# Two levels of Strassen for two of three feed-forward products, with their sums made during attention

## The chip, the core and the metric

The kernel runs on one core of a Trainium2 chip. The metric is the device time of one execution in microseconds, as the median of several runs. The program is one launch: inputs and output lie in HBM, everything between in the core's own memories (SBUF and PSUM) or in HBM scratch tensors of the kernel.

## What is computed

A transformer block with gated slot attention and a gated feed-forward part, on x of shape (2, 2048, 512), all in float32. Of the reference this matters here:

```python
x = layernorm(x + attention(x, Wq, Wk, Wv, Wg, Ws, Wo, g_norm_weight))
up_gate = einsum('bsd,hd->bsh', x, W1)      # W1: 2048 x 512
up_lin  = einsum('bsd,hd->bsh', x, W3)      # W3: 2048 x 512
hidden  = silu(up_gate) * up_lin
hidden  = fwht(hidden)                      # Walsh-Hadamard over the 2048 hidden channels
out     = einsum('bsh,dh->bsd', hidden, W2) # W2: 512 x 2048
x = layernorm(x + out)
```

The Hadamard transform is linear, so the kernel applies it once to W2 and leaves `hidden` as it is.

## The kernel before, in words

**Strassen's form.** A product of two matrices cut into 2 x 2 quarters needs eight products of quarters; Strassen's form (in Winograd's variant) needs seven, of quarters and of sums of quarters. Every large product here is made that way once. Each left factor is kept as seven slots (`LEFT`, line 91, says which slot product k reads), each right factor too (`RIGHT`), and `SUM` says in which of three PSUM sums product k is accumulated: products 1, 6, 7 and 4 go into c1, one after the other, and each of the partial sums on the way is read before the next product is added on top; 5 and 3 go into c2, 2 into c3. So product 6 may not start before the sum after product 1 was read, 7 not before that after 6, and 4 not before that after 7. In this document such a wait from one product of c1 to the next is a hop.

**Attention** (lines 114 to 672). Four groups of four heads (NG = 4), and in each group 16 steps of 128 tokens of both batch rows: 64 steps. `run(new, now, before, old)` (line 557) writes out one step's instructions by hand for TensorE (PE), VectorE (DVE), ScalarE (ACT) and GpSimd (POOL), under `manual_schedule`, so these four engines take their instructions in exactly this order. It interleaves four steps: `new` loads and (in the first group) transposes tokens (`load_x`, `make_x`), `now` makes q, k, s and v and the scores, `before` makes the values, `old` adds its output product to the residual rows (`o`, line 474), in the last group normalises them (`row_stats`, `store_rows`) and writes them to the HBM tensor yd. Transfers are issued by SyncE (SP), whose order a scheduler sets. PSUM has eight banks: `ps[0]` and `ps[1]` with two each for scores and transposes, and four for the sums of `Unit` (line 203): c1 twice, c2 and c3 once.

**W2's preparation** is a generator, `hadamard()` (line 505), which is advanced at three places of each step from the second group on: after `make_x`, after `row_stats`, and ahead of `store_rows`. It loads a tile, transposes it, multiplies it with a 128 x 128 Hadamard matrix, makes four stages of sums (`stage`, lines 516 and 517: two DVE additions of 1024 elements; one stage in every third place), forms Strassen's seven slots and stores them in the HBM tensors w2s.

**Feed-forward** (lines 675 to 860), under the scheduler's own order. Four blocks of eight row tiles (1024 tokens). `load_tokens` reads a block's rows from yd, transposes them and makes the seven slots. For each of eight pairs of hidden blocks, `up` makes W1's and W3's seven products each, with 512 columns (`product`, line 747), W1's and W3's turn about, so two chains of c1 alternate; ACT copies some sums (`keep`, line 754), DVE adds others (`add`, line 759), `combine` (line 764) makes the silu with a tanh on ACT and two DVE operations, and POOL makes the sums that W2's product needs. The weights' slots are made in the first block from W1 and W3 (`load_weights`, line 710, with transposes on PE) and kept in HBM (w13s); later blocks load them. `down` (line 799) makes W2's product for four pairs at a time, each of its seven products with four multiplications of 256 columns, and adds it to the residual rows (line 824), normalised after the second call.

Of the kernel before, what the change touches and what calls it, by code (L numbers as in the profile page):

```python
# [8 lines left out]
F32 = mybir.dt.float32  # L9
AF = mybir.ActivationFunctionType  # L10
ALU = mybir.AluOpType
# [15 lines left out]
NPB = NFB // 2  # L27
HD = D // 2
EPS = 1e-5
# [4 lines left out]
def gated_slot_attention_ffn_kernel(  # L34
# [20 lines left out]
    of = out.rearrange("b t d -> (b t) d")  # L55

# [38 lines left out]
    w13s = [dram.tile([P, 2, 7, 2, P], F32, name=f"w13s{p}") for p in range(NPB)]  # L95
# [15 lines left out]
    with ExitStack() as att:  # L111
        wp = att.enter_context(tc.tile_pool(name="wp", bufs=1))
        xp = att.enter_context(tc.tile_pool(name="xp", bufs=2))
        yp = att.enter_context(tc.tile_pool(name="yp", bufs=7))
# [28 lines left out]
        class Weights:  # L143


            def __init__(self, name, parts, raw=None):
                width = sum(p[1] for p in parts)
                self.t = wp.tile([P, 7, 2, width], F32, name=name)
# [36 lines left out]
        def load_o(g):  # L185
            def scaled(a):

                nc.gpsimd.tensor_scalar(a, a, gn, 0.5, ALU.mult, ALU.mult)

            at = g * HG * DV  # L190
            return Weights("wo_", [(lambda j: wo[at + 2 * j * DV : at + (2 * j + 2) * DV, :], HD)], scaled)

# [308 lines left out]

# [3 lines left out]
        def hadamard():  # L505

            for pair in ((0, 2), (1, 3)):
                wh = [hp.tile([P, NFB, P], F32, name=f"wh{i}") for i in range(2)]
                ping = hp.tile([P, NFB, P], F32, name="ping")

                def stage(i, s):

                    src, dst = (wh[i], ping) if s % 2 == 0 else (ping, wh[i])
                    a = src.rearrange("p (a two s) d -> p a two s d", two=2, s=1 << s)
                    o = dst.rearrange("p (a two s) d -> p a two s d", two=2, s=1 << s)
                    nc.vector.tensor_tensor(o[:, :, 0], a[:, :, 0], a[:, :, 1], ALU.add)
                    nc.vector.tensor_tensor(o[:, :, 1], a[:, :, 0], a[:, :, 1], ALU.subtract)

                for i, dt in enumerate(pair):
                    for q in range(NFB // 4):  # L520
                        raw = yp.tile([P, D], F32, name="raw", tag="rows")
                        nc.sync.dma_start(out=raw, in_=w2[dt * P : (dt + 1) * P, q * D : (q + 1) * D])
                        yield
                        for c in range(4):
                            nc.tensor.transpose(bank(0)[:, c, :], raw[:, c * P : (c + 1) * P], ident)
                        t0 = hp.tile([P, 4, P], F32, name="t0")
                        nc.scalar.copy(t0, bank(0))
                        yield
                        nc.tensor.matmul(bank(2), lhsT=hm, rhs=t0, start=True, stop=True)
                        nc.scalar.copy(wh[i][:, 4 * q : 4 * q + 4, :], bank(2))  # L530
                        yield
                for i in range(2):
                    for s in range(4):
                        stage(i, s)
                        for _ in range(3):
                            yield
                j = pair[0] * P
                for hb in range(NPB):
                    b11, b21, b12, b22 = (wh[i][:, hb + h * NPB] for i in range(2) for h in range(2))
                    wt = hp.tile([P, 4, P], F32, name="wt")  # L540
                    nc.vector.tensor_tensor(wt[:, 0], b12, b11, ALU.subtract)
                    nc.gpsimd.tensor_tensor(wt[:, 2], b22, b12, ALU.subtract)
                    nc.vector.tensor_tensor(wt[:, 1], b22, wt[:, 0], ALU.subtract)
                    nc.gpsimd.tensor_tensor(wt[:, 3], b21, wt[:, 1], ALU.subtract)
# [3 lines left out]
                    nc.sync.dma_start(out=o[:, 3:7], in_=wt)  # L548
                    yield
# [3 lines left out]
        w2_work = hadamard()  # L553
# [3 lines left out]
        def run(new, now, before, old):  # L557
# [23 lines left out]
            prepare = new is not None and new.g > 0  # L581
            if prepare:
                next(w2_work, None)
# [7 lines left out]
            if prepare:  # L591
                next(w2_work, None)
# [6 lines left out]
            if prepare:  # L599
                next(w2_work, None)  # L600
# [53 lines left out]
            if last:  # L654
                nw["qks"].sums(3)

        with tc.manual_schedule(
# [13 lines left out]
            for _ in w2_work:  # L671
                pass


    xp = ctx.enter_context(tc.tile_pool(name="fxb", bufs=1, reuse_waits="tile"))
    rawp = ctx.enter_context(tc.tile_pool(name="fraw", bufs=3, reuse_waits="tile"))
    hp = ctx.enter_context(tc.tile_pool(name="fhid", bufs=5, reuse_waits="tile"))
    wp = ctx.enter_context(tc.tile_pool(name="fw13", bufs=2, reuse_waits="tile"))
    w2p = ctx.enter_context(tc.tile_pool(name="fw2", bufs=4, reuse_waits="tile"))
    tmp = ctx.enter_context(tc.tile_pool(name="ftmp", bufs=2, reuse_waits="tile"))  # L680
    rp = ctx.enter_context(tc.tile_pool(name="fres", bufs=1, reuse_waits="tile"))
    ptp = ctx.enter_context(tc.tile_pool(name="ptp3", bufs=2, reuse_waits="tile", space=PSUM))
    pch = ctx.enter_context(tc.tile_pool(name="pch", bufs=2, reuse_waits="tile", space=PSUM))
    NBLK = NCH // 8
    TH = 4 * P
    GP = 4

    def load_tokens(blk):

        xb = xp.tile([P, 7, 2, TH], F32, name="xb")  # L690
        b12 = xp.tile([P, 2, TH], F32, name="b12")
# [207 lines left out]
```

## Time and profile before

| | us |
|---|---|
| median of three runs | 3827.41 (3825.83 to 3828.25) |
| the profiled execution | 3831.67 |
| its span, first to last instruction | 3829.9 |
| PE busy in the span | 3765.3 |
| DVE busy | 1983.0 |
| ACT busy | 966.5 |
| POOL busy | 806.4 |
| attention, from the start to its last PE product | 2608.5 |
| the rest, feed-forward | 1221.4 |

In a group's row of the profile stand the line, the engine, the operation, out<-in, the shapes and the count; then the busy time in us and the mean of one instruction in ns; then the time for which the engine was idle just ahead of these instructions, and what ended most of that wait. PE executes a float32 multiplication as two instructions, so each program-level multiplication is counted twice. In the chain of work in order of time, a line has the start, the length and the work; in the timeline, start, length and instruction, with the idle time and its releaser in brackets.

### The profile page before, as it was taken

Reading aid. Unit: us, or ns where it says so; the run is one execution under the profiler, and the core shown is the slowest. Engines: PE = TensorE matmul, PEld = TensorE weight load, DVE = VectorE, ACT = ScalarE, POOL = GpSimd, SP = SyncE. Lnnn points to the kernel's source line nnn. Section 1 sums busy time; section 2 is a strip of 40 time slices with the busy share of each in tenths; the row PEclk is TensorE's granted clock in tenths of the full one; section 3 lists DMA queues with packets and bytes.
Section 4 is the critical chain, followed back from the end, with each engine's and each line's share of the span. In section 5 each row is a group of like instructions: output and inputs, shape, how many; then the busy total and the mean of one; then the engine's idle time right before and its main releaser. Section 6 shows DMA issues by size and latency. Waiting matters only on the chain.

```text
span 3829.9 us, 57893 instructions
## 1 busy us (share of the span) xinstructions
PE 3765.3 (98%) x24416; PEld 2657.8 (69%) x24416; DVE 1983.0 (52%) x3020; ACT 966.5 (25%) x1621; POOL 806.4 (21%) x821
## 2 busy tenths in 40 slices
PE   9999999999999999999999999997999999999999
PEld 7777777677777777777777777774566466466466
DVE  5555555555655655546666666563434334334334
ACT  2322222222222222232222222222211211211211
POOL 2222221211212222112122222222311211212211
PEclk9999999999999999999999999998999999999999
DMA  4112113111121321111221211104323224223220
GB/s 142 56 53 79 53 57 107 60 57 59 42 74 48 100 79 48 60 59 42 74 88 63 78 53 61 47 25 170 121 88 124 77 77 143 77 77 119 93 77 22
DMA packets 124579, 290.19 MB, mean 76 GB/s; under 512 B 13600, under 2 KB 52640, under 8 KB 120224
## 3 DMA queue, kind: packets, MB, share of 16 engines
q1 hardware_dynamic: 124320, 286.50, 22.1%
q8 instruction: 192, 3.15, 0.3%
q14 instruction: 67, 0.55, 0.0%
HBM read 207.68 MB, written 78.64 MB: 75 GB/s over the span
## 4 chain that ended last, share of the span: by engine, by line
PE 94%; DVE 2%; DMA 1%; issue 1%; POOL 1%; ACT 0%; SPq 0%; POOLq 0%; DVEq 0%; ACTq 0%
PE c L301 20%; PE c L749 20%; PE c L271 16%; PE c L484 10%; PE c L817 9%; PE ps L427 3%; PE ps L363 2%; PE ps L410 2%; PE ps L348 2%; PE ps L468 1%; PE ps L329 1%; PE ps L415 1%; PE ps L433 1%; PE ps L351 1%; DMA raw<-in_L_ffn_W 1%
## 5 line engine op out<-in xcount | busy, mean ns | idle before, releaser
L301 PE MATMUL c<-wvg,xb 128*128 128x512 f32 x1792 | 863.8, 605 | 0.0
L749 PE MATMUL c<-xb,w 128*128 128x512 f32 x1792 | 776.3, 594 | 0.7 <-ACT w L725 0.7
L749 PEld LDWEIGHTS c<-xb,w 128*128 128x128 f32 x1792 | 339.6, 191 | 417.3 <-issue 406.9
L271 PE MATMUL c<-xb,wqks 128*128 128x128 f32 x3584 | 557.1, 278 | 7.0 <-DVE rows L480 2.0
L271 PEld LDWEIGHTS c<-xb,wqks 128*128 128x128 f32 x3584 | 491.1, 193 | 29.2 <-DVE rows L480 3.6
L301 PEld LDWEIGHTS c<-wvg,xb 128*128 128x128 f32 x1792 | 310.8, 190 | 266.4 <-issue 257.2
L817 PE MATMUL c<-w2t,hid 128*128 128x256 f32 x1792 | 392.5, 379 | 3.9 <-DVE res L824 3.9
L817 PEld LDWEIGHTS c<-w2t,hid 128*128 128x128 f32 x1792 | 338.3, 190 | 53.0 <-DVE res L824 6.3
L224 ACT COPY kept<-c 128x384 f32<-128x384 f32 (+1 forms) x384 | 203.0, 529 | 651.3 <-PE c L271 497.3
L271 PE MATMUL c<-wqks,xb 128*128 128x128 f32 x1792 | 348.5, 276 | 0.9 <-DMA wqks<-in_L_attn_Ws 0.9
L229 DVE TENSOR_TENSOR t<-c,kept 128x384 f32<-128x384 f32 (+1 forms) x384 | 230.4, 601 | 195.1 <-PE c L271 194.6
L761 DVE TENSOR_TENSOR out<-c,kept 128x512 f32<-128x512 f32 x192 | 131.7, 686 | 339.3 <-PE c L749 339.3
L480 DVE TENSOR_TENSOR rows<-c,rows 128x256 f32<-128x256 f32 x448 | 182.1, 417 | 188.3 <-PE c L484 186.6
L271 PEld LDWEIGHTS c<-wqks,xb 128*128 128x128 f32 x1792 | 273.7, 193 | 1.2 <-DMA wqks<-in_L_attn_Ws 1.2
L756 ACT COPY kept<-c 128x512 f32<-128x512 f32 x192 | 112.4, 585 | 599.0 <-PE c L749 599.0
L288 POOL TENSOR_TENSOR e<-e,zc 1x512 f32<-1x512 f32 x60 | 75.8, 1264 | 782.8 <-ACT e L287 782.8
L340 DVE RECIPROCAL iz<-z 128x256 f32<-128x256 f32 x128 | 223.6, 1747 | 20.9 <-ACT z L331 20.9
L824 DVE TENSOR_TENSOR res<-c,res 128x256 f32<-128x256 f32 x224 | 94.0, 421 | 232.6 <-PE c L817 232.6
L394 POOL TENSOR_TENSOR r<-r,iz 128x512 f32<-128x512 f32 x64 | 81.3, 1271 | 613.0 <-DVE sm L392 613.0
L440 DVE TENSOR_TENSOR t<-ps,t 128x1024 f32<-128x1024 f32 x64 | 78.3, 1224 | 239.0 <-ACT sq L438 239.0
L785 POOL TENSOR_TENSOR hid<-hid,a 128x512 f32<-128x512 f32 x32 | 40.7, 1273 | 704.4 <-DVE a L768 704.4
L388 ACT ACTIVATE r<-r 128x512 f32<-128x512 f32 x64 | 40.3, 630 | 458.8 <-DVE r L387 458.8
(164 smaller groups left out, 4795.1 us busy)
## 6 DMA issues: line engine op xcount, KB each, us to landing
xb<-xd SPq DMA_DIRECT2D x48, 896.0 KB, 4.7
w<-w13s SPq DMA_DIRECT2D x24, 1792.0 KB, 7.4
yd<-rows SPq DMA_DIRECT2D x128, 256.0 KB, 2.6
w2t<-w2s SPq DMA_DIRECT2D x32, 896.0 KB, 6.7
rows<-yd SPq DMA_DIRECT2D x96, 256.0 KB, 2.8
xd<-xb SPq DMA_DIRECT2D x16, 896.0 KB, 3.7
w13s<-w SPq DMA_DIRECT2D x8, 1792.0 KB, 5.7
raw<-in_L_ffn_W SPq DMA_DIRECT2D x48, 256.0 KB, 3.0
```

Source lines behind the costliest of these rows:

```text
L224: nc.scalar.copy(self.kept[k], s)
L229: nc.vector.tensor_tensor(t[:, to], s, self.kept[other], ALU.add)
L271: nc.tensor.matmul(out[:, i * P : (i + 1) * P], lhsT=a, rhs=b, start=(k in OPENS and c == 0 and i == 0), stop=(c == 1), skip_group_check=True,
L301: nc.tensor.matmul(out, lhsT=self.xb[:, RIGHT[k], c, :], rhs=w["vg"].t[:, LEFT[k], c, :], start=(k in OPENS and c == 0), stop=(c == 1), sk ...
L340: nc.vector.reciprocal(self.iz[:, h], self.z[:, h])
L427: nc.tensor.matmul(po[th, j, i], lhsT=self.a2[:, j, i, th], rhs=self.value(i, j), start=self.first, stop=True, skip_group_check=True,)
L480: nc.vector.tensor_tensor(y_, self.uo.sum(k), y_, ALU.add)
L484: nc.tensor.matmul(out, lhsT=self.ob[:, RIGHT[k], c, :], rhs=w["o"].t[:, LEFT[k], c, :], start=(k in OPENS and c == 0), stop=(c == 1), ski ...
L749: nc.tensor.matmul(s[i][SUM[k]], lhsT=w[:, i, LEFT[k], c, :], rhs=xb[:, RIGHT[k], c, :], start=(k in (1, 2, 5) and c == 0), stop=(c == 1), ...
L756: nc.scalar.copy(t, s[i][SUM[k]])
L761: nc.vector.tensor_tensor(t, s[i][c], kept[i][k], ALU.add)
L817: nc.tensor.matmul(s[SUM[m]], lhsT=hids[p][:, LEFT[m], k * P : (k + 1) * P], rhs=w[p][:, RIGHT[m], :], start=(m in (1, 2, 5) and p == 0), ...
```

## The change

- W1's and W3's products get a second level. A quarter product is itself cut into 2 x 2 and made by seven: 49 products in place of 64 (28 of 32 with one level), each with two multiplications of 256 columns. A *unit* is one of four sets of hidden blocks (`NSET`) in one of four token blocks, 16 units in all. Its outer products come in the order `OUTER`, the inner in `INNER`; the results of the inner seven are added into SBUF accumulators u, v, w and x (`acc`), by ACT copies where an accumulator starts and DVE additions elsewhere, and eight of the outer sums by POOL.
- `silu` has one tanh of 1024 elements per quarter of the result and four DVE pieces of 512, which `after` holds back for a number of slots; a slot is one product of either kind.
- W2's product for a unit (`down`, 28 products of two multiplications) is taken between the products of the next unit; `DOWNS` says how many belong to each outer product. The whole stage now has a hand-written order on PE, DVE, ACT and POOL.
- W1's and W3's seven-by-seven slots are made in attention (`up_weights`): transposes on PE, sums on DVE, stored in w13s. W2's preparation follows (`down_weights`); its Hadamard stages now come one in every place. The token slots of the first three blocks are made in the last group's steps (`rows_transposed`, `block`: sums on POOL and DVE), those of the last block in the feed-forward stage (`last_block`). There are now four places in a step, the fourth at its end.
- In the feed-forward stage, each outer product loads its weight slots (0.9 MB) one ahead.

The diff, cut to its core:

```diff
@@ attention @@
+        def first_sums(eng, dst, a11, a12, a21, a22):
+            eng.tensor_tensor(dst[:, 0], a21, a22, ALU.add)
+            eng.tensor_tensor(dst[:, 2], a11, a21, ALU.subtract)
+            eng.tensor_tensor(dst[:, 1], dst[:, 0], a11, ALU.subtract)
+            eng.tensor_tensor(dst[:, 3], a12, dst[:, 1], ALU.subtract)
+        def up_weights():
...
+            def inner(d, src, at, n):
+                t = hp.tile([P, 4, 2, P], F32, name="inner", tag="h3", bufs=4)[:, :, 0:n]
+                first_sums(nc.vector, t, *(src(r, c) for r in range(2) for c in range(2)))
+                o = d[:, at : at + n].rearrange("p m k t -> p k m t")
+                for c in range(2):
+                    nc.sync.dma_start(out=o[:, c], in_=src(0, c))
+                nc.sync.dma_start(out=o[:, 2], in_=src(1, 1))
+                for k in range(4):
+                    nc.sync.dma_start(out=o[:, 3 + k], in_=t[:, k])
...
+            for n, (p, i, half) in enumerate(todo):
+                next(rest, None)
+                yield
+                wt = both[:, n // 2 % 2]
+                tp = ps[1].rearrange("p q (c t) -> p q c t", t=P)
+                for q in range(2):
+                    for c in range(KC):
+                        nc.tensor.transpose(tp[:, q, c], raws[q][:, c * P : (c + 1) * P], ident)
+                nc.scalar.copy(wt[:, half].rearrange("p i a b t -> p i (a b) t"), tp)
+                next(rest, None)
+                yield
+                next(rest, None)
+                if half:
+                    outer = hp.tile([P, 4, 2, 2, P], F32, name="outer", tag="h2")
+                    first_sums(nc.vector, outer, *(wt[:, r, :, c] for r in range(2) for c in range(2)))
+                    rest = inners(w13s[p][:, :, :, i], wt, outer)
+                yield
...
+        def block(j):
...
+            t1, t2, t3, t4 = (tile_(f"y{k}") for k in (1, 2, 3, 4))
+            second_sums(nc.gpsimd, (t1, t2, t3, t4), b11, b12, b21, b22)
+            for m, src in enumerate((b11, b21, b22, t1, t2, t3, t4)):
+                if m == 3:
+                    yield
+                inner(m, src)
+                yield
...
-            prepare = new is not None and new.g > 0
-            if prepare:
-                next(w2_work, None)
+            y["second"] = new is not None and new.g > 0
+            next(pieces[0], None)
...
+            next(pieces[0], None)
+            if old is not None and old.g == NG - 1 and old.n < NCB - 4:
+                rows_transposed(old)
+                if old.n % 4 == 3:
+                    pieces[0] = block(old.n // 4)
@@ feed-forward @@
+    NU = NBLK * NSET
+    OUTER = (1, 2, 5, 3, 6, 7, 4)
+    DOWNS = (0, 8, 9, 4, 3, 2, 2)
+    INNER = (1, 5, 6, 2, 7, 3, 4)
+    BLOCK = {1: 0, 2: 0, 5: 3, 7: 3, 6: 1, 3: 1, 4: 2}
+    ENDS = (2, 7, 3, 4)
...
+        for n, slots in enumerate({11: (3, 6, 9, 12), 12: (5, 7, 9, 10), 22: (5, 7, 10, 11), 21: (3, 4, 5, 6)}[at]):
+            after(slots, lambda n=n: piece(n // 2, n % 2))
...
+        for i, m in enumerate(OUTER):
+            w, left, right = ws.pop(0), LEFT, xb[RIGHT[m]]
+            if i < 6 or u + 1 < NU:
+                ws.append(load_w(u + (i + 1) // 7, (i + 1) % 7))
...
+            c = sums(pup, 2 * TQ, "u")
+            for k in INNER:
+                s = c[SUM[k]]
+                for j in range(2):
+                    nc.tensor.matmul(
+                        s[:, j * TQ : (j + 1) * TQ], lhsT=w[:, LEFT[k], j, :], rhs=right[:, RIGHT[k], :],
+                        start=(k in (1, 2, 5) and j == 0), stop=True, skip_group_check=True,
+                    )
+                b = BLOCK[k]
+                if k in (1, 5, 6, 4):
+                    if first is None:
+                        nc.scalar.copy(t[to][:, b], s)
+                    else:
+                        add(t[to], s, b, t[first])
+                else:
+                    add(t[to], s, b)
+                if m in (6, 7) and k in ENDS:
+                    o = t["w" if m == 6 else "v"][:, b]
+                    nc.gpsimd.tensor_tensor(o, o, t["u"][:, b], ALU.add)
...
+        for at in (RIGHT[m] for m in OUTER):
+            load_x(0, at)
+        ws = [load_w(0, 0)]
+        h, last = None, last_block()
+        next(last)
+        for u in range(NU + 1):
+            now = {}
+            ups = up(u, now) if u < NU else iter(())
+            downs = down(u - 1, h) if u else iter(())
...
+            for n in range(49):
+                if u < NU:
+                    next(ups)
+                    slot()
+                    if n % (6 if u else 2) == 1 and n < (49 if u else 26):
+                        next(last, None)
+                i, k = divmod(n, 7)
+                while u and done < sum(DOWNS[:i]) + DOWNS[i] * (k + 1) // 7:
+                    next(downs)
+                    done += 1
+                    slot()
```

## The prediction

> **What bounds the kernel now.** I read the engines' busy shares first, then the chain of work that ended last, then the costliest groups.
>
> ```profile
> span 3829.9 us, 57893 instructions
> PE 3765.3 (98%) x24416; PEld 2657.8 (69%) x24416; DVE 1983.0 (52%) x3020; ACT 966.5 (25%) x1621; POOL 806.4 (21%) x821
> PE 94%; DVE 2%; DMA 1%; issue 1%; POOL 1%; ACT 0%; SPq 0%; POOLq 0%; DVEq 0%; ACTq 0%
> ...
> L749 PE MATMUL c<-xb,w 128*128 128x512 f32 x1792 | 776.3, 594 | 0.7 <-ACT w L725 0.7
> L817 PE MATMUL c<-w2t,hid 128*128 128x256 f32 x1792 | 392.5, 379 | 3.9 <-DVE res L824 3.9
> L761 DVE TENSOR_TENSOR out<-c,kept 128x512 f32<-128x512 f32 x192 | 131.7, 686 | 339.3 <-PE c L749 339.3
> L756 ACT COPY kept<-c 128x512 f32<-128x512 f32 x192 | 112.4, 585 | 599.0 <-PE c L749 599.0
> L824 DVE TENSOR_TENSOR res<-c,res 128x256 f32<-128x256 f32 x224 | 94.0, 421 | 232.6 <-PE c L817 232.6
> L785 POOL TENSOR_TENSOR hid<-hid,a 128x512 f32<-128x512 f32 x32 | 40.7, 1273 | 704.4 <-DVE a L768 704.4
> ```
>
> TensorE works 98% of the span and is 94% of the chain. An f32 multiplication has two records, so 1792 records are 896. DVE waits for PE in every group: behind each add there is room. Next the chain in order of time, for the length of an attention step (L484's stretch opens each one).
>
> ```profile
> 973.94 2.59 PE c L484 x12
> 1013.45 2.59 PE c L484 x12
> 1495.34 2.59 PE c L484 x12
> 1536.15 2.59 PE c L484 x12
> 2060.29 2.59 PE c L484 x12
> 2099.80 2.59 PE c L484 x12
> 3064.08 48.35 PE c L817 x224
> ```
>
> A step takes 39.51 us. One that also prepares a W2 tile (four transposes, one Hadamard product) takes 40.81. Those around 974 also have two 1.22 us Hadamard sums on DVE (L516, L517) and still take 39.51: DVE work of that size is free there. The last line is the second product's pace: 48.35 / 224 x 4 = 0.863 us for two multiplications of 256 columns, the unit of everything below. Last, the timeline, for two prices.
>
> ```profile
> 2573.95 0.73 POOL L200 TENSOR_TENSOR ob<-ob 128x256 f32<-128x256 f32 x1
> 2574.03 1.21 DVE L398 TENSOR_TENSOR r<-r,sm 128x512 f32<-128x512 f32 x1 [0.55 <-POOL r L394]
> ...
> 2578.05 0.42 DVE L480 TENSOR_TENSOR rows<-c,rows 128x256 f32<-128x256 f32 x1 [0.35 <-PE c L484]
> 2579.70 0.42 DVE L480 TENSOR_TENSOR rows<-c,rows 128x256 f32<-128x256 f32 x1 [1.22 <-PE c L484]
> 2580.27 0.45 PE L484 MATMUL c<-wo__13836,ob 128*128 128x256 f32 x1 [0.61 <-DVE rows L480]
> ```
>
> L398 has two SBUF inputs; alone such an operation takes 0.69 us (L387), beside a POOL operation 1.21. The other lines are products that share a PSUM sum, each waiting for the add that reads it: 1.74 us a round (2578.53 to 2580.27), which is 0.863 + 0.42 + 0.45 of signalling.
>
> **What the Trainium skill says.** "SBUF — State Buffer", Who interferes with whom: a DVE instruction with two SBUF inputs contends with a GpSimd instruction that reads SBUF, one that loses blocks until the other ends, and a DVE instruction with one SBUF input does not contend. The trace agrees on both: L398 above, while adds from PSUM (L728 at 2839.86) keep 0.42 us beside a POOL operation. "TensorE: Matmul & The Clock Gate", What's actually happening: the clock halves after an idle window of some 3.4 us. Here the granted clock is 1.0 but for a few windows, among them one from 2613 to 2633 us; stalls under 2 us, as below, should not reach it.
>
> **The change, part by part.** The reckoning is against the span of 3829.9 us; PE's last attention product ends at 2608.5, so the feed-forward stage takes 1221.4.
>
> *Products.* W1 and W3: 4 blocks x 8 pairs x 28 = 896 multiplications of 512 columns become 16 units x 49 x 2 = 1568 of 256. A unit has 49 of these products and 28 of W2's, (49 + 28) x 0.863 = 66.4 us with PE never waiting. W2's number stays (896). The first unit has no W2 products (42.3 us), and 28 of them, 24.2 us, come alone at the end.
>
> *Stalls in a unit.* Before, two chains of seven alternated with 1.72 us a product; now one chain runs, and c1 is written by products 1, 6, 7, 4 with one product (0.863) between. The next needs 0.69 (add) + 0.45: late by 0.25 us, with an ACT copy of 0.585 by 0.15. W2 products hide this where they lie between, but the distribution 0, 8, 9, 4, 3, 2, 2 leaves bare three hops in the first outer product, one in the fifth, two each in the sixth and seventh: 6 x 0.25 + 2 x 0.15, about 1.9 us. Then the silu pieces: 16 of 512 elements, 0.61 us start to start, 12 of them in the sixth, seventh and next first outer products. DVE there has seven adds (0.61), two of W2's (0.32) and four pieces, 7.35 us for PE's nine products, 7.77: nearly full, and in order. A slot of 0.863 has 0.25 beside an add, so a piece ahead of an add on which a hop waits costs 0.36; three lie so. With 0.5 for a first copy behind tanh on ACT (1.06 us): 1.5 us. Then the lock: POOL gets eight accumulator sums and eight hidden sums, 16 x 1.27 = 20 us a unit, mostly there, and pieces have two SBUF inputs. Followed product by product, about four wait some 0.4 us each for POOL: 1.6. The bounds are nothing (no meeting) and 12 x 0.64 = 7.7 (each meets half an operation). Sum: 66.4 + 1.9 + 1.5 + 1.6 = 71.4 us. The first unit, with 21 bare hops and pieces, has some 8 us of stalls and last_block's 32 transposes (3.5): 53.8.
>
> *Ends of blocks.* Row statistics and normalisation give DVE 2.8 us per row pair, four pairs a block, now between products: of 11 us I count 6 as seen, 18 for three blocks. Bounds 0 and 33.
>
> *Loads.* Per outer product 0.9 MB of w13s is fetched, one ahead. The page has 4.7 us for 0.9 MB and 7.4 for 1.8, so it fits the shortest stretch, 6.0 us, except where the next x tile lands with it: 3 us in all (0 to 25). The feed-forward tokens can come early, since their space is weights that attention has done with: a gap of 2 us, or 20 as now if they don't.
>
> *Attention.* Eight transposes cost 40.39 - 39.51 = 0.88 us (first-group steps against bare ones). W1 and W3: 16 steps x 0.88 = 14.1. Rows of three blocks: 12 x 0.88 = 10.6. W2's PE work is what it was. Sums: in a step, from the seventh output product's add to the q add that q's last product waits for, PE takes 8.4 us and DVE works 2.5 (5.2 in the last group, with statistics), so 5.9 (3.2) are free. W1/W3's sums fill 4.0 of 5.9: about 3 us in all for POOL's meetings. Hadamard stages come at all four places instead of one: 3 x 2.3 = 6.9, over by 1.0, and the one at the step's end delays the output's add by 1.6; four such steps, 10. In the last group each block's sums are 3 x 1.4 = 4.2 of 3.2, over by 1.0 in two steps, 0.6 at the end, and in the first step POOL's four sums of 1024 elements (1.9 us by L451) block DVE for 3.4: 6 us a block, 18. Nothing if they meet elsewhere, 45 if row statistics queue behind POOL too. SP gets 28 more transfers in two steps, at about 0.4 us of issue each: 11 of 79 us, behind which a load waits, but hidden, with steps' loads issued ahead.
>
> *Sum.* 2608.5 + 24.7 + 31 = 2664.2; gap 2; first unit 53.8; 15 x 71.4 = 1071; block ends 18; loads 3; last W2 products with the wait for silu 27; tail as now 8.7 (3821.2 to 3829.9): 3847.7. The median stands 2.5 under the profiled span: **3845 us**, 0.5% slower.
>
> **Rivals.**
> *Faster.* The sums and the lock are hidden: a unit costs only its hops, 68.3, attention 10 us of stalls instead of 31, the first unit 52, block ends 10. 2643.2 + 2 + 52 + 1024.5 + 10 + 3 + 27 + 8.7 = 3770.4: 3768. For it: free Hadamard sums at 974 and DVE's average of 76% in a unit. Against: order, not average, decides. The point is 70.2 us a unit: (3829.9 - 2776.7) / 15.
> *Late loads.* The gap of 20 remains and each unit's first outer product waits 1.5 us for weights: 3847.7 + 18 + 22 = 3888, so 3885. For it: SP in order with many new transfers; against: DMA engines at 22%.
> *It cancels.* Units at 70.2, within 0.2% (8 us, about what a measurement can tell).
>
> **Numbers.** Forecast 0.48 (3836 to 3875), faster 0.28, cancelled 0.12, late loads 0.12. The range reaches down to the faster case and past the late loads, 3765 to 3895. Faster by over 0.2% 0.28, within 0.12, slower 0.60.
>
> **What would show it.** Right: attention ends near 2664; a unit takes 71 to 72 us; PE's idle time lies before c1's products in the last two and first outer products, released by DVE; silu pieces of 0.69 read about 1 us. Wrong: units under 70 us, pieces at 0.69, steps of the last group at 40.4, or PE released by DMA.

## The result, and the profile after

| | before | after |
|---|---|---|
| median of the runs, us | 3826.6 | 3909.8 (3909.1 to 3913.6) |
| span of the profiled execution | 3829.9 | 3907.4 |
| attention, to its last PE product | 2608.5 | 2664.5 |
| feed-forward part | 1221.4 | 1242.9 |

The changed kernel takes 1.0219 of the time before (95% interval 1.0201 to 1.0237): 83 us more, where 18 were forecast. The sign was right, the size not.

The page of the changed kernel, the same parts as were shown of before:

```profile
span 3907.4 us, 62432 instructions
PE 3729.3 (95%) x25760; PEld 2921.6 (75%) x25760; DVE 2523.9 (65%) x3936; ACT 918.3 (24%) x1461; POOL 1002.4 (26%) x929
PE 80%; DVE 12%; POOL 4%; issue 3%; ACT 1%; DMA 1%; SPq 0%; POOLq 0%; DVEq 0%; ACTq 0%
...
L915 PE MATMUL uc<-xb,w 128*128 128x256 f32 x3136 | 788.7, 391 | 98.9 <-DVE acc_u L898 89.8
...
L951 PE MATMUL dc<-w2t,hid 128*128 128x256 f32 x1792 | 459.2, 385 | 8.4 <-DVE res L958 6.1
```

With its fewer products PE is busy 36 us less than before, and yet the span is 77.5 us longer: the chain was PE for 94% and is PE for 80%, with DVE at 12%. The row of W1's and W3's products shows where: PE stood idle for 98.9 us just ahead of them, 89.8 of these because of the adds of L898. The mean of a W2 multiplication is 385 ns, 379 before: part of the time the clock was halved (626 ns in those windows, 379 outside).

Where the sum of the forecast and the trace part (starts of the units' first products, up to the span's end):

| term | forecast | measured |
|---|---|---|
| end of attention | 2664.2 | 2664.5 |
| gap, then first unit | 2 + 53.8 | 0 + 63.7 |
| units 2 to 15, with block ends and loads | 14 x 71.4 + 21 = 1020.6 | 1061.7 |
| last unit, last W2 products, tail | 71.4 + 27 + 8.7 = 107.1 | 117.5 |

All of the miss of 60 us in the span lies in the feed-forward part: 8, 41 and 10 us. (In the median it is 65: the forecast put the median 2.5 us under the profiled span, and it stands 2.4 over it.) The chain of work in order of time shows attention, where the forecast's total held; here the first step of the last group that has a block's sums in it:

```profile
2201.60 2.59 PE c L492 x12
...
2211.21 2.49 DVE halves L527
2213.71 2.51 DVE halves L528
...
2249.49 0.65 PE c L492 x3
```

The step takes 47.89 us (2201.60 to 2249.49) in place of 40.39; two DVE sums that take 0.42 us elsewhere take 2.5 while POOL makes its sums of 1024 elements, and they end in the chain. The three blocks cost 8.2, 8.6 and 6.3 us over two steps each (23 where 18 were forecast), W1's and W3's sums and the Hadamard stages 8 where 13 were.

Next the timeline of one first outer product, the worst place of a unit. Columns: start, length, instruction, and in brackets the idle time before it and what ended it.

```profile
3186.98 1.65 POOL L881 TENSOR_TENSOR hid<-a,hid 128x512 f32<-128x512 f32 x1 [1.56 <-DVE hid L877]
3187.53 1.64 DVE L877 TENSOR_TENSOR hid<-hid,acc_u 128x512 f32<-128x512 f32 x1
3188.71 1.60 POOL L882 TENSOR_TENSOR hid<-hid 128x512 f32<-128x512 f32 x1
3189.10 1.75 DVE L875 SCALAR_TENSOR_TENSOR hid<-hid,acc_u 128x512 f32<-128x512 f32 x1
3190.27 1.71 POOL L884 TENSOR_TENSOR hid<-hid 128x512 f32<-128x512 f32 x1
3190.78 0.68 DVE L898 TENSOR_TENSOR acc_u<-uc,acc_u 128x512 f32<-128x512 f32 x1
3191.38 1.15 DVE L877 TENSOR_TENSOR hid<-hid,acc_u 128x512 f32<-128x512 f32 x1
3192.45 1.27 DVE L898 TENSOR_TENSOR acc_u<-uc,acc_u 128x512 f32<-128x512 f32 x2
...
3193.18 1.99 PE L915 MATMUL uc<-xb,w 128*128 128x256 f32 x8 [2.48 <-DVE acc_u L898]
```

Silu's pieces (L875, L877) and POOL's sums (L881 to L884) take turns. The sum that began at 3186.98 ends at 3188.63, the piece 0.54 later at 3189.17, the next sum at 3190.31, the next piece at 3190.85: a round of 1.68 us, in which DVE does 0.68 us of work. An add with its input in PSUM (3190.78) keeps its 0.68, but the adds stand behind such pieces in DVE's queue, and PE waits 2.48 us for them. Elsewhere a stall of this kind is followed by something that the forecast had excluded. Two stretches of an earlier unit; columns: the stretch, its length, busy time of PE, PEld, DVE, ACT and POOL with counts, the granted clock, the DMA share, GB/s.

```profile
2806.50:2809.20 2.70, 0.00 (x0) 0.00 (x0) 2.70 (x4) 0.00 (x0) 0.81 (x1) 1.00 0.65 160
2809.20:2816.00 6.80, 6.28 (x23) 5.33 (x24) 3.35 (x7) 0.59 (x1) 1.27 (x1) 0.75 0.66 242
```

PE stands still for 3.43 us (from 2806.29), and for half of the stretch after it the clock is 0.5. Counted from the second unit on, 12 of the 15 first outer products leave a window of 3.4 or 6.8 us at half clock: with the two at the end 66 us of half clock.

The first outer product is the worst place, but not the only one. Just ahead of the one shown above, in the seventh outer product of the unit before it:

```profile
3179.34 1.06 ACT L871 ACTIVATE hid<-acc_v 128x1024 f32<-128x1024 f32 x1 [10.12 <-POOL acc_v L929]
3180.43 0.69 DVE L875 SCALAR_TENSOR_TENSOR hid<-hid,acc_v 128x512 f32<-128x512 f32 x1 [0.56 <-ACT hid L871]
...
3183.31 1.13 PE L915 MATMUL uc<-xb,w 128*128 128x256 f32 x4 [0.78 <-DVE acc_u L898]
```

This piece keeps its 0.69 us. It is late because the tanh is, and the tanh waits for POOL's last sum of an accumulator; the adds behind it are late too. So POOL's sums cost PE time in two ways: they stretch pieces, and their own results come late.

### The profile page after: what moved, and what is told of

Its sections match the earlier page's. It is cut to its first block, busy times and chain, and to the rows that moved or that the text cites. A ratio compares the mean times of both kernels' runs of the same rounds, so it can differ in the third digit from the quotient of the medians.

```text
span 3907.4 us, 62432 instructions
## 1 busy us (share of the span) xinstructions
PE 3729.3 (95%) x25760; PEld 2921.6 (75%) x25760; DVE 2523.9 (65%) x3936; ACT 918.3 (24%) x1461; POOL 1002.4 (26%) x929
## 4 chain that ended last, share of the span: by engine, by line
PE 80%; DVE 12%; POOL 4%; issue 3%; ACT 1%; DMA 1%; SPq 0%; POOLq 0%; DVEq 0%; ACTq 0%
PE c L309 19%; PE c L279 14%; PE uc L915 12%; PE c L492 9%; PE dc L951 8%; PE ps L435 3%; POOL acc_v L929 2%; PE ps L371 2%; PE ps L356 2%; DVE acc_u L898 2%; PE ps L418 1%; PE ps L337 1%; PE ps L441 1%; PE ps L359 1%; PE ps L476 1%
## 5 line engine op out<-in xcount | busy, mean ns | idle before, releaser
L915 PE MATMUL uc<-xb,w 128*128 128x256 f32 x3136 | 788.7, 391 | 98.9 <-DVE acc_u L898 89.8
L915 PEld LDWEIGHTS uc<-xb,w 128*128 128x128 f32 x3136 | 596.1, 194 | 226.6 <-DVE acc_u L898 129.0
L951 PE MATMUL dc<-w2t,hid 128*128 128x256 f32 x1792 | 459.2, 385 | 8.4 <-DVE res L958 6.1
L951 PEld LDWEIGHTS dc<-w2t,hid 128*128 128x128 f32 x1792 | 346.4, 194 | 60.8 <-DVE res L958 9.1
L898 DVE TENSOR_TENSOR acc_u<-uc,acc_u 128x512 f32<-128x512 f32 x384 | 257.9, 684 | 78.4 <-PE uc L915 69.5
L296 POOL TENSOR_TENSOR e<-e,zc 1x512 f32<-1x512 f32 x60 | 75.8, 1263 | 823.9 <-ACT e L295 823.9
L958 DVE TENSOR_TENSOR res<-dc,res 128x256 f32<-128x256 f32 x448 | 188.1, 421 | 118.4 <-PE dc L951 112.0
L348 DVE RECIPROCAL iz<-z 128x256 f32<-128x256 f32 x128 | 223.7, 1747 | 20.3 <-ACT z L339 20.3
L929 POOL TENSOR_TENSOR acc_w<-acc_w,acc_u 128x512 f32<-128x512 f32 x64 | 80.8, 1286 | 529.5 <-DVE acc_u L898 528.7
L364 DVE TENSOR_TENSOR a<-ps,causal 128x1024 f32<-128x1024 f32 x64 | 78.3, 1224 | 149.4 <-PE ps L356 139.2
L435 PEld LDWEIGHTS ps<-t,a 128*64 128x64 f32 x2048 | 110.5, 137 | 50.5 <-DVE e L291 46.3
```

The lines of the kernel that those rows point to most:

```text
L348: nc.vector.reciprocal(self.iz[:, h], self.z[:, h])
L435: nc.tensor.matmul(po[th, j, i], lhsT=self.a2[:, j, i, th], rhs=self.value(i, j), start=self.first, stop=True, skip_group_check=True,)
L898: nc.vector.tensor_tensor(into[:, b], s, (into if first is None else first)[:, b], ALU.add)
L915: nc.tensor.matmul(s[:, j * TQ : (j + 1) * TQ], lhsT=w[:, LEFT[k], j, :], rhs=right[:, RIGHT[k], :], start=(k in (1, 2, 5) and j == 0), st ...
L951: nc.tensor.matmul(s, lhsT=h["hid"][:, i, LEFT[m], k * P : (k + 1) * P], rhs=h["w2"][:, i, RIGHT[m], :], start=(m in (1, 2, 5) and i == 0) ...
L958: nc.vector.tensor_tensor(r, s, r, ALU.add)
```

## The experiments

**My theory** after this reading: the lock between DVE and POOL makes silu's pieces two to three times as long where they meet; the adds behind them are late; the stall halves the clock. **The rivals**: DVE's queue is too long there whatever POOL does; the ends of blocks; the hops. A unit is counted from first product to first product. A *quiet* unit has no end of a block and no half clock in it; before any edit it takes 72.8 us (the average of all units is 75.8), and where one figure is given for a unit of another run, it is the quiet one.

**POOL's sixteen sums of a unit write without reading** (e1_no_lock).

```diff
-nc.gpsimd.tensor_tensor(hid[:, i, 5], hid[:, i, 0], a21[:, i], ALU.subtract)
+nc.gpsimd.memset(hid[:, i, 5], 0.5)
```

and so the seven like it of a unit, and L929.

> The changed kernel with POOL's sixteen sums of a feed-forward unit replaced by memsets of the same tiles: the sums are left out, POOL's place in the order stays, but POOL reads nothing. Theory of the lock: silu's DVE pieces, which have two SBUF inputs, no longer wait for POOL; L875 and L877 fall to 0.68 us everywhere, the first outer product from 9.0 to about 7 us, the sixth and seventh from 9.4 to 8.6 to 9.0, with the short stalls the half-clock windows go, and a unit falls from 75.8 to about 71: some 75 us in all, near 3835. Theory of the queue (the pieces overfill DVE whatever POOL does): the first outer product stays near 9 us, the gain is under 15 us, near 3900.

Measured: 3818.4 us (3811.6 to 3826.9, a wider spread than in the other runs), 0.997 (0.9956 to 0.9984) of before. The groups of instructions of the changed kernel between 2900 and 3650 us, then of this one:

```profile
L877 DVE TENSOR_TENSOR a<-a,acc_w 128x512 f32<-128x512 f32 x20 | 28.0, 1400 | 0.0
...
L875 DVE SCALAR_TENSOR_TENSOR hid<-hid,acc_u 128x512 f32<-128x512 f32 x20 | 24.2, 1209 | 0.0
L877 DVE TENSOR_TENSOR hid<-hid,acc_u 128x512 f32<-128x512 f32 x20 | 23.2, 1159 | 0.3
```

```profile
L877 DVE TENSOR_TENSOR a<-a,acc_w 128x512 f32<-128x512 f32 x22 | 15.0, 682 | 0.0
...
L877 DVE TENSOR_TENSOR hid<-hid,acc_u 128x512 f32<-128x512 f32 x20 | 13.7, 686 | 0.3
...
L875 DVE SCALAR_TENSOR_TENSOR hid<-hid,acc_u 128x512 f32<-128x512 f32 x20 | 13.6, 679 | 0.0
```

These three groups, six of a unit's sixteen pieces, go from 1.16 to 1.40 us back to 0.68 (the other ten took 0.68 to 0.78), a quiet unit from 72.8 to 68.4, and half clock from 66 to 22 us. Of the 4.4 us of a quiet unit the first outer product gives 2.2 (9.01 to 6.77), the sixth and the seventh 1.1 each. So 91 us hang on POOL's sixteen sums: more than the theory asked, and all of the slowdown. That they read SBUF is not the only difference here: a memset takes 0.53 us where a sum took 1.27 or more, so POOL's results are early too, and the wait for the tanh shown above is gone with the lock.

**Silu without DVE's pieces** (e2_no_pieces): the sixteen pieces of a unit are not issued.

> The changed kernel without silu's DVE pieces (the hidden values are the bare tanh; the product with gate and lin is left out). Both theories: no piece stands ahead of an add, so what is left over 66.4 us of a unit is the hops of c1: 1.9 us, the first outer product 6.6, the fifth 8.8, the sixth and seventh 8.3 us, no half-clock windows; a unit at 68.3 and near 3795. If the hops cost more than 0.25 us each, or the half-clock windows stay, the unit stays over 70 and the time over 3825.

Measured: 3796.7, 0.9917 (0.9903 to 0.9932), a unit of 68.03. With 66.4 of pure products the hops cost 1.6 us. Beside e1_no_lock this says that the same pieces, unlocked, cost a unit only 0.4.

**Ends of the first three blocks without statistics and normalisation** (e3_no_ends), and **the same work in pieces** (e13_ends): one row at a time, in slots of its own in the next unit.

```diff
-rows = [(res[i, k], i * NCB + blk * 4 + k) for i in range(2)]
-stats = [row_stats(t) for t, _ in rows]
+for i in range(2):
+    finish_row(res[i, k], i * NCB + blk * 4 + k, (1 if blk == NBLK - 1 else (1, 1, 36, 10)[k]) + 2 * i)
```

`finish_row` makes one row's statistics in slot d and its normalisation in slot d + 3.

> The changed kernel without row statistics and normalisation in the first three blocks (they are left out; the last block has them). If the ends of blocks cost what was reckoned, 6 us each, and half-clock windows that follow the longest stalls another 1 to 2 each: 20 to 25 us less, near 3887. If that work is hidden between the products: under 6 us less, near 3905. If it is what trips the clock in all units: 40 less, near 3870.

> Statistics and normalisation of the eight rows that end a block are put in pieces of one row into slots of the next unit's outer products that DVE has room in, in place of two rows at once. The kernel without them for three blocks took 18.6 us less than the changed kernel. If the cost is the burst of two rows on DVE ahead of the adds, most of that comes back, some 10 to 15 us: 3895 to 3900. If DVE's work as such is the cost, nothing comes back: 3908 to 3912.

Measured: 3891.2 (1.0165, 1.015 to 1.0181) and 3890.7 (1.0161, 1.0146 to 1.0177). The ends cost 18.6 us (the half clock that follows them included), and put in pieces they cost nothing that can be measured: it was the place, not the work.

**Three unread products ahead of product 4 of each first outer product** (e5_fill), 2.6 us of PE work where PE would stand still.

```diff
+                if i == 0 and u and k == 4:
+                    f = pdn.tile([P, HD], F32, name="fill", tag="c3")
+                    for _ in range(6):
+                        nc.tensor.matmul(f, lhsT=w[:, 0, 0, :], rhs=right[:, 0, :], start=True, stop=True)
```

> The changed kernel with three products more (six multiplications of 256 columns, 2.6 us, that nobody reads) on PE in each first outer product from the second unit on, ahead of product 4, where PE stands still for 2.65 us waiting for DVE. Theory of the clock (the stall trips the clock gate and the products after it run at half clock): the stall is filled, costs nothing itself, and the half-clock windows behind it go, with 1 to 2 us of each unit: 15 to 20 us less, near 3892. If PE's stall is not waiting for DVE, or the windows come from elsewhere: 15 x 2.6 = 39 us more, near 3949. If the windows stay and the stall is filled: the same 3910.

Measured: 3890.6 (1.0162, 1.0146 to 1.0177). Half clock falls from 66 to 17.8 us, the first outer products stay at 9.0 us, the second come down from 14.3 to 12.95. Useless work made the kernel 19 us faster: this is the clock's part, 1.2 us a unit.

**Pieces of the last quarter (21) later**, where W2's products lie between (e6_slots), and **silu by ACT's own function** in place of the tanh, with two pieces for a quarter in place of four (e7_silu).

```diff
-22: (5, 7, 10, 11), 21: (3, 4, 5, 6)
+22: (5, 7, 10, 11), 21: (8, 10, 12, 14)
```

```diff
-nc.scalar.activation(o, gate, AF.Tanh, scale=0.5)
+nc.scalar.activation(o, gate, AF.Silu)
...
-nc.vector.scalar_tensor_tensor(o[:, i], o[:, i], 1.0, gate[:, i], ALU.add, ALU.mult)
...
-nc.vector.tensor_tensor(o[:, i], o[:, i], lin[:, i], ALU.mult)
+nc.vector.scalar_tensor_tensor(o[:, i], o[:, i], 2.0, lin[:, i], ALU.mult, ALU.mult)
```

> The changed kernel with the silu pieces of the last quarter (21) at slots 8, 10, 12, 14 instead of 3, 4, 5, 6: behind POOL's sums of the quarter before, in the second outer product, where DVE has room. All work is kept. Theory of the lock: the first outer product falls from 9.0 to about 7 us, most half-clock windows go, the second outer product stays near 12.95; a unit falls from 75.8 to 72 to 73, near 3860. Rival, the wait moves: the pieces meet POOL's sums of slot 6 there, or W2's fourth and sixth products wait for the late hidden values; then the second outer product grows by 2 us or more and the time stays over 3895.

> The changed kernel with silu made whole by ACT's Silu function instead of tanh, so that a quarter needs two DVE pieces instead of four (each with two SBUF inputs still), at slots (3, 9), (5, 9), (5, 10), (4, 6). POOL's sums stay. Theory of the lock: each piece is a meeting with POOL, half of them go; the first outer product near 7.5 us, the sixth and seventh near 8.8, a unit at 71 to 72, near 3850. If POOL's rhythm and not the number of pieces sets the wait (one meeting delays DVE as much as two): over 3885.

Measured: 3850.2 (1.0056, 1.0041 to 1.0071) and 3839.9 (1.003, 1.0019 to 1.0042), 60 and 70 us off with POOL's sums untouched; both more than expected. In e6_slots the first outer product takes 6.52 us, the second 12.95, and half clock is 15 us. Its groups of the pieces that were moved, in the same stretch as above:

```profile
L875 DVE SCALAR_TENSOR_TENSOR hid<-hid,acc_u 128x512 f32<-128x512 f32 x20 | 16.1, 806 | 0.0
L877 DVE TENSOR_TENSOR hid<-hid,acc_u 128x512 f32<-128x512 f32 x20 | 13.6, 678 | 0.0
```

They took 1.21 and 1.16 us. So the moved pieces are not stretched at a place where it costs little; they hardly meet POOL's sums any more. The sixth and seventh outer products, which nothing was done to, still take 9.39 and 9.37 us. In e7_silu half of the pieces are gone, and those of the groups that met POOL still take 1.14 and 1.16 us each.

**The last block's transposes from the 15th product on** (e8_last_late), for the first unit.

```diff
-if n % (6 if u else 2) == 1 and n < (49 if u else 26):
+if n % (6 if u else 2) == 1 and (u or 14 <= n < 40):
```

> The changed kernel with last_block's transposes in the first unit begun at its 15th product instead of its second. If PE's 15.2 us in the first outer product (6 if it never waited) are a wait for the rows that these transposes need, which come behind 6.4 MB of token slots: 6 to 8 us less, near 3903. If it is the first products' own loads: no change, 3910.

Measured: 3911.3 (1.0217, 1.0202 to 1.0233), the first outer product still 14.8 us, and the first unit 68.5. That rival fell; the timeline of the changed kernel names another:

```profile
2667.59 1.31 SPq L505 DMA_DIRECT2D yd<-rows  x2
...
2672.21 1.07 ACT L922 COPY acc_u<-uc 128x512 f32<-128x512 f32 x2 [17.50 <-DMA rows<-yd]
...
2672.85 3.58 PE L915 MATMUL uc<-xb,w 128*128 128x256 f32 x8 [4.70 <-ACT acc_u L922]
```

The first copy into an accumulator starts only after transfers on attention's row tiles, whose memory the accumulators take over; PE waits 4.7 us for it, and half clock comes with it (2669.3 to 2676.1). **The FFN's pools in another order** (e16_pools), so that the accumulators lie elsewhere and no instruction changes:

```diff
-    ap_ = ctx.enter_context(tc.tile_pool(name="facc", bufs=4, reuse_waits="tile"))
-    hp = ctx.enter_context(tc.tile_pool(name="fhid", bufs=2, reuse_waits="tile"))
-    w2p = ctx.enter_context(tc.tile_pool(name="fw2", bufs=2, reuse_waits="tile"))
     rp = ctx.enter_context(tc.tile_pool(name="fres", bufs=1, reuse_waits="tile"))
+    w2p = ctx.enter_context(tc.tile_pool(name="fw2", bufs=2, reuse_waits="tile"))
+    hp = ctx.enter_context(tc.tile_pool(name="fhid", bufs=2, reuse_waits="tile"))
+    ap_ = ctx.enter_context(tc.tile_pool(name="facc", bufs=4, reuse_waits="tile"))
```

> The FFN's six SBUF pools are opened in another order, so that the accumulators lie at the end and the residual rows lie where the accumulators were; no instruction is changed. If the first unit is late (63.7 us, 53.8 forecast) because ACT's first copies into the accumulators wait for the store of attention's last rows out of the same memory, the first unit loses most of its 6 us stall and the half clock after it: about 55 us, and the kernel about 3901 to 3903. If the wait belongs to something else (the first weights' arrival, the end of attention's own chain), the first unit stays at 63 us and the time at 3910.

Measured: 3901.9 (1.0188, 1.0171 to 1.0205). In its timeline the same copy, right behind its product:

```profile
2665.81 0.59 ACT L922 COPY acc_u<-uc 128x512 f32<-128x512 f32 x1 [10.87 <-PE uc L915]
```

The first outer product falls from 15.24 to 8.69 us, the first unit from 63.7 to 59.5, where about 55 was expected (some of the gain is lost to later waits in it, among them 1.44 and 1.19 us for weights), and 7.9 us come off the whole. The total meets its forecast although the first unit gave only 4.2 us; the trace has 2 more in the units after it.

**The block's four sums in attention without reading** (e9_block): POOL's `second_sums` replaced by four memsets.

> The changed kernel with POOL's four sums of a token block in attention's last group replaced by memsets of the same tiles (the sums are left out; DVE's sums of them and the transfers stay). Three steps take 47.9, 48.3 and 46.9 us instead of 40.4. If, as predicted, DVE's own sums are over its room by 1 us and the rest is POOL's lock: 41.4 us a step, 19 us less in all, near 3891. If DVE's own sums are most of it: 45 us or more a step, under 9 us less, over 3900.

Measured: 3893.0 (1.0169, 1.0152 to 1.0186); the first steps of the three blocks are 41.1, 42.5 and 41.2 us in place of 47.9, 48.3 and 46.9.

**All of POOL's sums of a unit on DVE** (e14_dve), those of the hidden blocks one or two slots after their piece: nothing is left out, and none of the sixteen is left on POOL for a piece to meet.

> All sums are still made and read, but the sixteen of a unit that POOL made (eight of the hidden blocks, eight of the accumulators) are made by DVE: those of the accumulators at once, those of the hidden blocks one and two slots after the piece that they need. POOL then has no operation that takes two SBUF operands in the units. If what was paid was the alternation of DVE's and POOL's two-operand operations on SBUF, the pieces go back to 0.68 us, DVE gets 16 x 0.68 = 10.9 us of work more per unit (72% of a unit busy now, some 85% then), a unit takes about 70 us in place of 75.8, and the kernel about 3830. If what was paid is the order and the amount of DVE's queue, the same pieces stand in the same slots with sixteen operations more among them, and the time is 3910 or over.

Measured: 3949.5 (1.0315, 1.0301 to 1.033): slower than the change itself. My number fell, and its reason half. Every piece is 0.68 us, as the lock would have it; the first outer product goes from 9.31 to 8.48 and the second from 14.32 to 12.95. But the seventh goes from 9.37 to 12.98: with seven adds (0.69), two of W2's (0.42), four pieces and four hidden sums (0.68) DVE has there, worked out, 11.1 us of work for PE's nine products, 7.77. Half clock rises to 90 us. So both limits are real: what POOL does not do, DVE must, in the same tight places.

**The edits together**: silu, slots and block ends (e11_both); the same with all POOL sums, attention's too, on DVE (e15_all); and the first with the other order of the pools (e17_best).

```diff
-{11: (3, 6, 9, 12), 12: (5, 7, 9, 10), 22: (5, 7, 10, 11), 21: (3, 4, 5, 6)}
+{11: (3, 9), 12: (5, 5), 22: (6, 10), 21: (8, 10)}
```

> Three edits together, POOL's sums left as they are: silu by ACT's own function with two DVE pieces for a quarter, the last quarter's pieces in slots of the second outer product, and the block ends in pieces of one row. Alone, the first gave 70 us and the second 60. What is paid is one stall in each first outer product (2.65 us, and half clock after it), which either edit takes away, so the two overlap: about 3820 with 10 to 15 us of block ends, that is within 0.3% of the kernel before. If they were independent costs, 3910 - 70 - 60 - 15 = 3765.

> The three edits of silu, slots and block ends, and with them all of POOL's sums on DVE: the sixteen of a unit, and the four sums of a transform block in attention. If the lock between DVE and POOL is what is left in both parts, a unit comes to about 67.5 to 68 us and the block steps lose some 5 of their 8 us: about 3795 to 3805, faster than the kernel before by 0.6 to 0.8%. If DVE becomes the bound with them, a unit stays at 70 us or over: 3825 or more, and the version with POOL's sums is the faster of the two.

> The version with silu by ACT's own function, later slots and block ends in pieces (3805.5), and with it the pools in the other order. If the first unit's stall is one of memory and has nothing to do with the other three edits, its 8 us come off in full: 3797 to 3799. If another wait takes its place at the attention's end, 3803 to 3806.

Measured: 3805.5 (0.9938, 0.9925 to 0.995), 3865.0 (1.0095, 1.0081 to 1.0109) and 3795.1 (0.9911, 0.9896 to 0.9926). The first saves 104 us; its parts alone saved 60 + 70 + 19, so at least 45 us were one and the same: the stall of the first outer product and the half clock behind it, which either of two edits removes. (At least, since the slots of two other quarters moved as well, and the seventh outer product, 9.43 us in e7_silu, takes 8.49; that the forecast was 15 us too high may come from there.) In this run no group of silu's pieces takes more than 0.69 us, with POOL's sums all in place. e15_all fell: units of 71.8 in place of 68.5, and the block steps still take 47.4 to 48.4. Those four sums cost the step on DVE what they cost on POOL: four times 1.22 us of work on DVE, or, in the changed kernel, two DVE sums held up by 2.1 us each. e17_best adds the pools, 10.4 us more, a little over the 8 expected. It beats the kernel before by 0.9%. One unit's length of it, then the same of the changed kernel, columns as above:

```profile
3400.00:3468.50 68.50, 68.17 (x309) 57.86 (x308) 44.26 (x77) 8.85 (x12) 20.34 (x17) 1.00 0.49 175
```

```profile
3400.00:3474.50 74.50, 69.67 (x315) 58.81 (x313) 54.28 (x88) 8.85 (x12) 23.33 (x17) 1.00 0.33 112
```

POOL does the same sums in 20.3 us that took 23.3, DVE is busy 10 us less, and PE does a unit's work in 68.5. From its page:

```profile
PE 3703.4 (98%) x25760; PEld 2905.0 (77%) x25760; DVE 2390.1 (63%) x3808; ACT 919.6 (24%) x1462; POOL 978.0 (26%) x929
```

PE is back at 98% of the span, as before the change, with less to do.

## Why the prediction was wrong in size, step by step

- *Products*: 66.4 us a unit. Right: the rate of 0.863 us a product holds wherever nothing waits (12.95 us for the 15 of the second outer product).
- *Hops*, "about 1.9 us" (the terms as written add up to 1.8): right, 1.6 (e2_no_pieces).
- *Pieces*, 1.5 us: too high, 0.4 without the lock.
- *The lock*, "about four wait some 0.4 us each for POOL: 1.6". **This is the step that failed first.** It let a piece meet POOL at most for part of a sum, as separate accidents. In the trace six pieces of a unit are stretched, by 3.5 us in all, since the two engines fall into turns, a round of 1.68 us for each piece as long as both have work; and half of the cost lands where four pieces and four sums lie in one outer product with no W2 product to cover it. POOL's sums measure 4.4 us in a quiet unit (72.83 - 68.4), inside the bounds of nothing and 7.7 that the forecast had set. Some 0.8 of the 4.4 is not the lock on a piece but the late tanh in the seventh outer product, which the forecast had nowhere. "SBUF — State Buffer", Who interferes with whom, in the Trainium skill, had the rule that the instruction that loses is blocked until the other ends, and the trace agrees (a DVE sum of 0.42 us took 2.5); what was missing was to follow the queue behind it.
- *The clock*, "stalls under 2 us, as below, should not reach it". **This term was put at nothing, and failed too**: the stalls came to 2.48 us and more, and by e5_fill their half clock costs 19 us. "TensorE: Matmul & The Clock Gate", What's actually happening, puts the gate at an idle window of some 3.4 us; the measurement is less kind and decides: of eight stalls of 2.48 us, six were followed by half clock, beginning 2.7 to 3.9 us after the stall did. The kernel before had shown it as well: of its three stalls of 2.67 us, those at 1363.82 and 2010.41 were followed by half clock. Why six and not the other two can be read off the trace. All 21 half-clock windows of the changed kernel start on one grid of 3.413 us, to within 0.001 us. Here are two windows of the grid with a part of such a stall in them, each followed by the next window (PE's busy time comes first, the clock behind POOL's):

```profile
2959.41:2962.82 3.41, 1.42 (x7) 1.27 (x8) 2.53 (x4) 0.25 (x1) 2.06 (x2) 1.00 0.44 185
2962.82:2966.23 3.41, 3.41 (x10) 2.66 (x9) 1.45 (x3) 0.33 (x1) 0.00 (x0) 0.50 0.78 255
...
3191.49:3194.91 3.42, 1.73 (x8) 1.55 (x9) 2.23 (x3) 0.56 (x1) 1.76 (x2) 1.00 0.34 143
3194.91:3198.32 3.41, 3.41 (x18) 3.00 (x17) 2.23 (x4) 0.03 (x1) 0.00 (x0) 1.00 0.85 282
```

  PE stands still for 1.99 us of the first, and half clock follows; for 1.7 us of the other, and it does not: 0.8 us of that stall lie in the window before. In the changed kernel every window at full clock with 1.99 us or more of standstill is followed by half clock, and none with 1.88 or less; in the kernel before the border lies between 1.97 and 2.02, in the other runs between 1.7 and 2.0. So here it is not the length of a stall alone that decides, but how much of it falls into one window.
- *First unit*, 53.8: 63.7. Some 4 to 8 of the 10 us are the memory of attention's rows (59.5 in e16_pools; 56.9 in e17_best against 64.5 in e11_both), a wait that the forecast did not look for: it asked what a new tile is computed from, not what lay in its place.
- *Ends of blocks*, 18: right, 18.6. *Loads*, 3: from the second unit on no product waits for a transfer, by the groups of waits; the late-loads rival fell. *Gap*, 2: none.
- *Attention*, 2664.2: right in total at 2664.5, by errors that cancel, which is luck: blocks 23 for 18 (POOL's sums of 1024 elements take 2.35 us each, where the forecast had 1.9), sums and stages 8 for 13.
- *The end*, 35.7 after the last unit: PE waits twice there,

```profile
3868.26 0.70 PE L951 MATMUL dc<-w2t,hid 128*128 128x256 f32 x2 [2.07 <-POOL hid L881]
3872.49 7.74 PE L951 MATMUL dc<-w2t,hid 128*128 128x256 f32 x23 [3.52 <-DVE res L958]
```

  5.6 us where 2.8 were counted, and half clock from 3870.8 for 6.8 us.

The 41 us of units 2 to 15 are thus about half the unit itself and half the clock. A quiet unit takes 72.83 us where 71.4 were forecast, 20 us in 14 units: POOL's sums 2.8 more than counted, pieces and hops 1.4 less, which hid half of the error by luck. Most of the other 21 is the 19 us of half clock. The first miss of the table is mostly the first unit's memory, the last one the same lock, waits and clock at the end. Of the signs that were to show the forecast right, the place held: PE waits before c1's products in the last two and the first outer products (3173.96, 3183.31, 3193.18 in the unit shown), released by DVE. The faster rival's unit, 68.3 us with sums and lock hidden, is what the better versions come to (68.5): it named the state the change can reach, not the one it was in. The range ended at 3895, 15 us short, because the upper bound of the lock (7.7) was not carried into it: 6.1 us more in 15 units would have reached it.

What stays open: the rest of the first unit's 10 us, of which the waits for weights in e16_pools are 2.6; and how the 91 us of e1_no_lock divide among the sixteen sums, and between the stretched pieces and POOL's late results, which were only taken away together.

## What to carry to other kernels

DVE and POOL, where both read two operands from SBUF, did not slow each other here by chance meetings but took turns as long as both had work: count rounds, and then ask which adds stand behind them and whether anything covers PE there. Before moving such work to the free engine, move it in time, to where the other engine has nothing to read: that took 60 us off with no work removed, while giving it all to DVE cost 40 more. And ask of each stall not only how long it is, but whether it trips the clock: a wait of 2.48 us did so in six of eight cases. When a stage takes over memory, the first write into a tile can wait for the last transfer that used it, as here for 4.7 us of PE's time, so the tiles that are needed first should lie where nothing was busy last.

## What the runs showed that I had not expected

- Three products that nobody reads, put into a stall, made the kernel 19 us faster, since PE's clock stayed up.
- Sums of 1024 elements on POOL (2.35 us each) and on DVE (1.22 us each) cost an attention step about the same, 6.5 to 8 us over 40.39: POOL's hold DVE up for about as long (twice 2.1 us) as DVE needs to make them (four times 1.22).
- Whether a stall of 2.48 us was followed by half clock depended on where it lay on a fixed grid of 3.413 us.
- The order in which six pools are opened was worth 8 to 10 us with the instructions unchanged.
